# A later issue of block ends while the last chunk's exponentials are made, in a four-layer graph network

## The chip, the core and the metric

The kernel runs on one core of one Trainium2 chip. The metric is the device time of one execution in microseconds. Beside it stands one profiled execution, with the start, the length and the waits of every instruction. Engines are named as in the profile: PE is TensorE (PEld its weight loads), DVE is VectorE, ACT is ScalarE, POOL is GpSimd, and SP is SyncE, which here only issues transfers.

## What is computed

Four layers of a graph network run over 2708 nodes with 512 features. The adjacency matrix is sparse: about 16 neighbours in a row of 2708. Each layer ends in `x = layernorm(x + layer(x))`. Layers 0, 1 and 3 are products with the adjacency and a weight. Layer 2 is the one that matters here. It is two attention layers in a row:

```python
def _gat_layer(x, W, adj):
    proj = x @ W
    Wh, Ws = jnp.split(proj, 2, axis=-1)
    scores = Wh @ Ws.T
    a = jax.nn.softmax(scores, axis=-1) * adj
    out = a @ Wh
    out = out + x
    return jax.nn.leaky_relu(out, NEG_SLOPE)

for l in range(W_stack.shape[0]):
    x = _gat_layer(x, W_stack[l], adj)
```

## The kernel before

**Blocks and chunks.** The 2708 rows are cut into 22 blocks of 128 rows (the last has 20). They are worked on in six chunks, of four, four, four, four, three and three blocks. The attention of one chunk (a `Chunk`, named by attention layer and number, such as 1_3 for chunk 3 of the second attention layer) goes through these stages:

- *Scores* (tiles `sp`, `s`): for each of the 22 blocks of neighbours, PE multiplies a 128-row block against the chunk's columns; ScalarE copies the result, VectorE keeps the running maximum (`top`).
- *Shift* (`shift_rows`, `shift_columns`): the maximum of each column is spread over the partitions by transposes.
- *Softening* (`soften`, steps v = 0 to 22): VectorE subtracts the shift from block v and ScalarE takes the exponential. In the same call, for block v - 1, VectorE adds to the sum (`sum`), multiplies with the mask (`a`), and SyncE writes the result into a table in memory (`pairs`) beside the projected rows. For the last chunk a step is three VectorE operations of 128 x 276.
- *List sums* (`fetch`, `weigh`): since a row has few neighbours, the product with the masked exponentials is made from lists. GpSimd gathers 128 table rows for one list by an indirect transfer (tile `g`), and PE multiplies the gathered weights with the gathered rows into one PSUM bank (`acc`). A full block has twelve lists: four single ones, and eight in two groups of four (quads), each list of a quad on a quarter of the columns. Gathers run at most ten lists ahead in eleven buffers, and each product frees its buffers. A chunk's gathers begin when its softening is issued in full.
- *End* (`end`): VectorE scales the bank by the reciprocal sum, adds the row (`xr`), applies the leaky relu (`r`). In the first attention layer SyncE then writes the row, and 8 us after a chunk's last end its four blocks are turned by PE transposes (`turn`) and written. In the second attention layer VectorE adds the layer's own input and takes the statistics, five operations in all; 2 us after a chunk's last end comes `normalize`, and 4 us later the rest of it, which puts the rows into `made`.

**The order of issue.** Every engine's order is fixed by the order in which the program issues (class `Ordered`). The attention is planned while the program is written out. `Attention.clock` is the planner's clock: each piece of PE work advances it by an assumed cost (4 x columns / 2400 us for a product, 0.853 us for a single list, 1.1 for a quad). `later(us, what)` puts a call into `pending`, to be run by the first `advance` that reaches its time. A list product is issued by `weigh()` when its gather is thought to have landed, or at once with `weigh(True)`. In the main loop of `layer` softening of one chunk is mixed with the scores of the next and with list products of the chunk before that.

**The last chunk.** When a layer's scores are all issued, only the last chunk's shift and softening are left, with list products of chunks 3 and 4. After each softening step `until(done, fill)` issues list products, or pieces of `fill`, until the clock reaches the step's time. For the first attention layer `fill` is the next one's projection (`second`: tiles `mix`, `wst`, `z`). For the second it is the start of layer 3 (`Fast.early`): products `acc<-m,xh` and `acc<-m,xl` in groups of four blocks. For these, `prepare` makes the mask copies `m` and the two halves `xh`, `xl` of each row on ScalarE and VectorE. At its second piece that fill asks for rows 12 to 15 with `need(15)`:

```python
def need(self, i):

    while i not in self.made:
        if not self.weigh(True):
            self.pending.pop(0)[1]()
```

Rows 12 to 15 are chunk 3; blocks 16 to 18 are chunk 4, blocks 19 to 21 chunk 5. After group 3 of a chunk of layer 3, the four banks are copied out by ScalarE (`begun`), and the next chunk's group 0 uses those banks.

Of the kernel before, what the change touches and what calls it, by code (L numbers as in the profile page):

```python
# [53 lines left out]
class Ordered:  # L54


    def __init__(self, tc):
        self.tc, self.last = tc, {}
        for name in ("tensor", "vector", "scalar", "gpsimd", "sync"):
            setattr(self, name, OrderedEngine(self, getattr(tc.nc, name)))  # L60
# [27 lines left out]
class Kernel:  # L88
# [129 lines left out]
    def attention(self, before, after):  # L218

        nc, tc, small = self.nc, self.tc, self.small  # L220
        with ExitStack() as ctx:
# [100 lines left out]
            for layer in range(2):  # L322
                w = self.load_w(wpool, self.w2[layer], 2 * D, f"w_2{layer}")
                for i in range(NB):
                    ps = self.transposed(ps_tr, x[i], f"x{i}")
                    xt = turned.tile([P, DC, P], FP, tag="t", name=f"xt{i}")
                    nc.scalar.copy(xt, ps)
                    ws = rows.tile([P, D], FP, tag="row", name=f"ws{i}")
                    nc.vector.tensor_copy(ws, self.times_w(ps_mm, xt, w, D, f"ws{i}"))
                    nc.scalar.copy(z[i], self.times_w(ps_mm, xt, w, 0, f"wh{i}"))  # L330
                    n = rows_of(i)
                    ps = self.transposed(ps_tr, ws, f"ws{i}")
                    nc.vector.tensor_copy(wst[:, :, i * P : i * P + n], ps[:, :, :n])

                mx = scores(0)
                rden = softmax(0, mx)
                for i in range(NB):
                    if i + 1 < NB:
                        mx = scores(i + 1)
                    acc = weigh(i)  # L340
                    finish(i, acc, rden, layer == 1)
                    if i + 1 < NB:
                        rden = softmax(i + 1, mx)


    def general(self):
# [106 lines left out]

        given = [self.x_in[bass.ts(i, P), :] for i in range(NB)]
        layer(0, given, self.w0, None, self.b0, end0)
        layer(1, self.saved[0], self.w1, dis, self.b1, end1)
        self.attention(self.saved[1], self.saved[2])
        layer(3, self.saved[2], self.w3, None, self.b3, end3)

    def other_weights(self):  # L460
# [27 lines left out]
def cost(columns):  # L488

    return 4 * columns / 2400  # L490
# [894 lines left out]
class Attention:  # L1385
# [7 lines left out]
    def __init__(self, fast):  # L1393
        self.f, self.k, self.nc = fast, fast.k, fast.nc
        self.page, self.bank = fast.page, fast.bank
        tc = self.k.tc
        self.scratch = self.k.ctx.enter_context(
            tc.tile_pool(name="pairs", bufs=1, space=DRAM)
        )

        self.pairs = [
            [
                self.scratch.tile([NP, 2 * PAIR + D], FP, tag=f"p{a}{b}", name=f"pairs{a}{b}")
                for b in range(2)
            ]
            for a in range(2)
        ]
        self.mixed = self.scratch.tile([DC, P, D], FP, tag="mixed", name="mixed")  # L1410
        self.layers = [AttentionLayer(a, self.pairs[a]) for a in range(2)]
        self.clock, self.fetch_free, self.pending = 0.0, 0.0, []


    def blank(self):
# [316 lines left out]
    def weigh(self, wait=False):  # L1732

        nc = self.nc
        self.fetch_ahead()
        ch = next((c for c in self.chunks if c.to_weigh), None)
        if ch is None:
            return False
        q, ts, first, last = ch.to_weigh[0]
        if len(ch.fetched) < len(ts):  # L1740
            return False
        if ch.fetched[len(ts) - 1][1] > self.clock and not wait:
            return False
        ch.to_weigh.pop(0)
        if ch.rden is None:
            self.divisor(ch)
        w = ch.blocks[q][2]
        gs = [ch.fetched.pop(0)[0] for _ in ts]
        if first:
            ch.acc = self.bank(1, f"acc{ch.name}_{q}")  # L1750
        for h, g in enumerate(gs):
            lo, m = (0, w) if len(gs) == 1 else (h * QW, QW)
            e, z = (0, P - lo) if q % 2 else (D + lo, 0)
            nc.tensor.matmul(
                ch.acc[lo : lo + m],
                g[:, e : e + m],
                g[:, z : z + D],
                start=first,
                stop=last,
            )  # L1760
        self.advance(cost(D) if len(gs) == 1 else 1.1)
        if last:
            a = (ch, q, ch.acc, ch.x.pop(q), ch.first.pop(q, None))
            self.later(1.5, lambda: self.end(*a))
        self.fetch_ahead()
        return True

# [59 lines left out]
    def layer(self, ly, chunks, fill):  # L1827
        f = self.f
        self.chunks, self.made = chunks, {}
        for k, ch in enumerate(chunks):  # L1830
            old = chunks[k - 1] if k else None


            js = [0, 1, 2, NB - 1, *range(3, NB - 1)]
            for n, j in enumerate(js):
                if old and n == 0:
                    self.load_masks(old)
                if old and n >= 3:
                    if n == 3 and k >= 3:
                        while chunks[k - 3].to_weigh:  # L1840
                            self.weigh(True)
                    for _ in range(1 + n % 2):
                        if old.softened <= NB:
                            self.soften(old)
                self.scores(ch, j)
                f.beat()
                if n == 14 and k:
                    f.packed(k - 1)
                if n == 4 and k + 1 < len(chunks):
                    self.load_moving(chunks[k + 1])  # L1850
                if k + 1 == len(chunks) and n in ((5, 11, 19) if ly.number == 0 else (5, 11)):
                    next(fill)
                if old and n == 0:
                    self.greatest(old, js[-1])
                if n:
                    self.greatest(ch, js[n - 1])

                for _ in range(3):
                    if not self.weigh():
                        break  # L1860
                if old and n == 1:
                    self.shift_rows(old)
                if old and n == 2:
                    self.shift_columns(old)
        last = chunks[-1]
        self.load_masks(last)
        self.greatest(last, js[-1])
        self.until(self.clock + 3, fill)
        self.shift_rows(last)
        if ly.number == 1:  # L1870

            next(fill)
        self.until(self.clock + 3, fill)
        self.shift_columns(last)

        done = self.clock + (2 if ly.number == 0 else 4)
        while last.softened <= NB:
            self.soften(last)
            done += 1.4
            self.until(done, fill)  # L1880
        while any(c.to_weigh for c in chunks):
            if not self.weigh() and not next(fill, False):
                assert self.weigh(True)
        while self.pending:
            if not next(fill, False):
                self.pending.pop(0)[1]()
        for _ in fill:
            pass
# [97 lines left out]
```

## Time and profile before

| what | us |
|---|---|
| median of three timed runs | 2321.81 |
| lowest and highest of them | 2318.35, 2332.58 |
| the profiled execution's own time | 2299.72 |
| its span, first to last instruction | 2297.7 |
| PE busy in the span | 2269.4 |
| DVE busy | 1391.5 |
| POOL busy | 705.4 |
| ACT busy | 675.5 |

The profiled execution is shorter than the timed ones. Nearly every group of instructions shows the same line, L71, since the helper that fixes the order issues them all, so groups are told apart by their tiles (`out<-in`). The last softening of the first attention layer lies at about 1263 to 1302 us of the span, that of the second at about 1957 to 2017 us.

### The profile page before, as it was taken

What the parts mean: (1) busy time and instruction counts of PE and PEld (TensorE: products, weight loads), DVE (VectorE), ACT (ScalarE), POOL (GpSimd) and SP (SyncE); (2) the same over time, 40 slices, a digit from 0 to 9 for tenths busy, and PEclk for the clock granted to TensorE, in tenths of its full rate; (3) what the DMA queues carried; (4) which work ended last, traced back from release to release, by engine and by line L of the source; (5) the groups of instructions that cost most, each with busy time, mean ns of one, the idle gap of its engine ahead of it and who ended that gap; (6) DMA issues with size and microseconds to landing.
All of it is one profiled execution on the core that took longest, in us unless ns stands there. A gap on an engine that the chain in (4) does not pass through costs nothing.

```text
span 2297.7 us, 25903 instructions
## 1 busy us (share of the span) xinstructions
PE 2269.4 (99%) x8525; PEld 1289.0 (56%) x8525; DVE 1391.5 (61%) x2803; ACT 675.5 (29%) x1354; POOL 705.4 (31%) x822
## 2 busy tenths in 40 slices
PE   9999999999999999999999999999999999899997
PEld 6776876777644444443555444444443555466685
DVE  6777787786553537748667511238769788525523
ACT  7444452322111123223322200113223334342211
POOL 3433431111000001635557540001635467442000
PEclk9999999999999999999999999999999999999999
DMA  9966752223547415858789997405868799963311
GB/s 351 286 188 184 199 168 81 76 81 104 208 184 267 144 25 184 303 191 297 254 311 360 349 412 284 183 8 179 303 218 286 254 322 339 334 217 120 116 51 43
DMA packets 260929, 486.34 MB, mean 212 GB/s; under 512 B 40238, under 2 KB 126950, under 8 KB 260784
## 3 DMA queue, kind: packets, MB, share of 16 engines
q1 hardware_dynamic: 192128, 269.63, 33.6%
q0 software_dynamic: 68656, 214.96, 28.0%
q8 instruction: 69, 1.13, 0.2%
q14 instruction: 76, 0.62, 0.1%
HBM read 307.55 MB, written 176.92 MB: 211 GB/s over the span
## 4 chain that ended last, share of the span: by engine, by line
PE 86%; DMA 6%; DVE 4%; ACT 1%; issue 1%; POOL 1%; SPq 0%; ACTq 0%; POOLq 0%; DVEq 0%
PE sp L71 33%; PE acc L71 30%; PE mm L71 8%; PE z L71 6%; PE wst L71 6%; DMA x<-x 2%; DMA x<-in_x 1%; DMA at<-in_adj_t 1%; DMA g<-pairs,givers 1%; PE mix L71 1%; DMA pairs<-s 1%; POOL xt L71 1%; PE list L71 1%; ACT m L71 1%; PE tr_x2t L71 0%
## 5 line engine op out<-in xcount | busy, mean ns | idle before, releaser
L71 PE MATMUL sp<-xs,wst_sb 128*128 128x512 f32 (+3 forms) x2112 | 798.3, 544 | 0.0
L71 POOL DMA_INDIRECT g<-pairs,givers x510 | 524.2, 1028 | 872.9 <-issue 338.9
L71 PEld LDWEIGHTS sp<-xs,wst_sb 128*128 128x128 f32 (+1 forms) x2112 | 379.7, 186 | 408.4 <-issue 324.8
L71 PE MATMUL acc<-m,xh 128*128 128x512 f32 (+4 forms) x1584 | 566.8, 379 | 6.6 <-ACT m L71 5.1
L71 PE MATMUL acc<-m,xl 128*128 128x512 f32 (+4 forms) x1584 | 549.6, 365 | 2.0 <-DVE xl L71 1.8
L71 PEld LDWEIGHTS acc<-m,xh 128*128 128x128 f32 (+1 forms) x1584 | 288.0, 188 | 70.9 <-issue 21.3
L71 PEld LDWEIGHTS acc<-m,xl 128*128 128x128 f32 (+1 forms) x1584 | 288.3, 188 | 46.3 <-issue 5.3
L71 PE MATMUL acc<-g 128*32 128x512 f32 (+1 forms) x1020 | 264.8, 606 | 4.6 <-DMA g<-pairs,givers 4.0
L71 ACT COPY s<-sp 128x512 f32<-128x512 f32 (+2 forms) x252 | 132.7, 528 | 396.8 <-PE sp L71 395.1
L71 ACT ACTIVATE s<-s 128x512 f32<-128x512 f32 (+3 forms) x264 | 151.6, 580 | 319.8 <-DVE s L71 319.5
L71 DVE TENSOR_TENSOR top<-top,s 128x512 f32<-128x512 f32 (+2 forms) x240 | 149.1, 621 | 156.1 <-ACT s L71 154.5
L71 PE MATMUL mm<-w,ht 128*128 128x512 f32 (+1 forms) x528 | 223.7, 593 | 0.0
L71 ACT CAST m<-at 128x512 fp32r<-128x512 uint8 (+5 forms) x396 | 199.2, 567 | 62.3 <-DMA at<-mask 19.7
L71 DVE TENSOR_TENSOR s<-s,shift 128x512 f32<-128x512 f32 (+3 forms) x264 | 162.7, 620 | 36.2 <-ACT shift L71 36.2
L71 DVE TENSOR_TENSOR s<-s,a 128x512 f32<-128x512 f32 (+3 forms) x264 | 165.8, 628 | 13.6 <-DMA a<-mask 4.5
L71 DVE TENSOR_TENSOR sum<-sum,s 128x512 f32<-128x512 f32 (+4 forms) x252 | 156.5, 621 | 15.4 <-ACT s L71 15.4
L71 PEld LDWEIGHTS mm<-w,ht 128*128 128x128 f32 (+1 forms) x528 | 95.8, 186 | 117.0 <-issue 112.2
L71 PEld LDWEIGHTS acc<-g 128*32 128x32 f32 (+1 forms) x1020 | 74.6, 134 | 148.0 <-issue 116.5
L71 PE MATMUL z<-w,xt 128*128 128x512 f32 (+1 forms) x352 | 151.0, 596 | 0.0
L71 PE MATMUL wst<-xt,mixed 128*128 128x512 f32 (+2 forms) x384 | 150.5, 544 | 0.0
L71 POOL DMA_DIRECT2D x<-o x44 | 26.0, 597 | 329.7 <-DVE o L71 325.4
L71 PEld LDWEIGHTS wst<-xt,mixed 128*128 128x128 f32 x384 | 72.0, 190 | 71.1 <-issue 58.8
(168 smaller groups left out, 1476.7 us busy)
## 6 DMA issues: line engine op xcount, KB each, us to landing
pairs<-z_sb SPq DMA_DIRECT2D x84, 768.0 KB
pairs<-s SPq DMA_DIRECT2D x168, 256.0 KB
at<-in_adj_t SPq DMA_DIRECT2D x84, 256.0 KB
xres<-x POOLq DMA_DIRECT2D x44, 256.0 KB, 4.6
x<-o POOLq DMA_DIRECT2D x43, 256.0 KB, 3.4
pairs<-s SPq DMA_DIRECT2D x84, 128.0 KB
x<-x SPq DMA_DIRECT2D x37, 256.0 KB
at<-mask SPq DMA_DIRECT2D x32, 256.0 KB
```

Source lines behind the costliest of these rows:

```text
L71: ins = call(*args, **kw)
```

## The change

A flag `ending` is set when a layer's scores are all issued, and cleared when the last softening step of the last chunk is issued. While it is set, the end of a block is put 7 us of the planner's clock behind the block's last list product instead of 1.5. A product counts by the moment at which it is issued.

```diff
         self.clock, self.fetch_free, self.pending = 0.0, 0.0, []
+        self.ending = False
...
         if last:
             a = (ch, q, ch.acc, ch.x.pop(q), ch.first.pop(q, None))
-            self.later(1.5, lambda: self.end(*a))
+
+            self.later(7 if self.ending else 1.5, lambda: self.end(*a))
         self.fetch_ahead()
...
-        last = chunks[-1]
+        last, self.ending = chunks[-1], True
         self.load_masks(last)
...
             self.until(done, fill)
+        self.ending = False
         while any(c.to_weigh for c in chunks):
```

## The prediction

> **What bounds the kernel now.** I read the page first: busy shares and the chain that ended last.
>
> ```profile
> span 2297.7 us, 25903 instructions
> PE 2269.4 (99%) x8525; PEld 1289.0 (56%) x8525; DVE 1391.5 (61%) x2803; ACT 675.5 (29%) x1354; POOL 705.4 (31%) x822
> PE 86%; DMA 6%; DVE 4%; ACT 1%; issue 1%; POOL 1%; SPq 0%; ACTq 0%; POOLq 0%; DVEq 0%
> ```
>
> TensorE is the bound, 86% of the last chain; what takes nothing from it or its waits is free. Then the two places where the flag is on, by busy time in stretches (the first numbers are the stretch, its length and PE's busy time).
>
> ```profile
> 1240.00:1310.00 70.00, 69.75 (x228) 32.37 (x227) 37.59 (x90) 17.84 (x41) 41.01 (x42) 1.00 1.01 358
> 1958.40:1978.10 19.70, 16.45 (x34) 3.51 (x33) 6.96 (x17) 5.33 (x9) 14.82 (x17) 1.00 1.03 413
> 1992.80:2001.40 8.60, 4.52 (x10) 2.34 (x9) 7.24 (x17) 5.88 (x12) 2.73 (x5) 0.64 0.59 172
> 2001.40:2008.80 7.40, 5.93 (x26) 4.55 (x24) 6.53 (x17) 4.36 (x10) 1.00 (x1) 0.96 0.82 254
> ```
>
> In the first attention layer (ending at 1251 to 1302 us) PE never waits. In the second (1943 to 2017) it does. In 1958.4 to 1978.1 it runs 16 lists (the 33 weight loads, two for each list) in 19.7 us, 1.23 each, as gathers land; its order of weight loads shows the cause:
>
> ```profile
> 1964.64 0.14 PEld L71 LDWEIGHTS acc<-g 128*32 128x32 f32 x2 [0.85 <-DMA g<-pairs,givers]
> 1966.42 0.14 PEld L71 LDWEIGHTS acc<-g 128*32 128x32 f32 x2 [1.65 <-DMA g<-pairs,givers]
> 1967.57 0.14 PEld L71 LDWEIGHTS acc<-g 128*32 128x32 f32 x2 [1.00 <-DMA g<-pairs,givers]
> ```
>
> GpSimd issues a gather every 1.26 us there (0.95 and a gap of 0.30), so PE goes at GpSimd's pace. VectorE meanwhile stands at the end of block 16, the first of chunk 4; its second line is the wait:
>
> ```profile
> 1961.74 0.17 DVE L71 TENSOR_SCALAR rs_v<-mv 128x4 f32<-128x4 f32 x1
> 1974.11 0.75 DVE L71 SCALAR_TENSOR_TENSOR xr<-acc,rden,xr 128x512 f32<-128x512 f32 x1 [12.20 <-PE acc L71]
> 1996.74 0.69 DVE L71 SCALAR_TENSOR_TENSOR xl<-x,xh 128x512 fp32r<-128x512 f32 x1 [0.18 <-ACT xh L71]
> ```
>
> Behind it stand the second softening step (1984.08) and everything after. PE pays later, at the fourth group of the next layer's products, and before the next chunk:
>
> ```profile
> 1997.27 0.80 PE L71 MATMUL acc<-m,xh 128*128 128x512 f32 x1 [4.08 <-ACT m L71]
> 2008.79 0.50 PE L71 MATMUL acc<-m,xh 128*128 128x512 f32 x1 [1.47 <-ACT begun L71]
> ```
>
> [...] one end held VectorE 12.20 us with ready softening behind it. [...] behind the 4.08 us gap the granted clock averages 0.64 over 8.6 us. Gather waits of at most 2.1 us set off nothing.
>
> **The change part by part.** An end is one scheduled call on the planner's clock, which I followed by hand from the costs in the code; it does not advance that clock. So weighing and filling keep their order unless somebody waits for the end itself. Five ends are registered while the flag is on.
>
> *First attention layer: two ends.* The last of chunk 3 (1270.61 us, two VectorE operations, 1.4 us) goes some five softening steps down, and its turn, 8 later, goes from 655.7 to 660.9 on the clock (it is run at the first advance past its time). With it move 16 transposes (1.9 us of PE), 4 ScalarE copies, one row DMA and four turned DMAs of SyncE, past some ten pairs writes. They are read only when that chunk is projected, over 50 us later on the clock. The end of chunk 4's first block goes from 1302.28 to about 1312, behind two copies of z. Neither end stalled VectorE before, and PE is full with fill: zero gained. One bank fewer is free at the turn, which could hold PE for a ScalarE copy (0.6): I take +0.3, bounds 0 and 1.
>
> *Second attention layer: three ends, and a loop that waits for one.* The fill calls `need(15)` in mid-ending. That loop forces list products until block 15's row is made: its end, 2 later the normalizing, 4 later the rest. With 0 at block 15's last product, a single list advances 0.853, a quad 1.1:
> - Before: end due 1.5, run at 1.71; normalizing due 3.71, run at 4.51; rest due 8.51, run at 9.02. That is 4 singles, 2 quads, 4 singles: the 16 lists of the trace.
> - After: end due 7, run at 7.32; normalizing due 9.32, run at 10.12; rest due 14.12, run at 14.64. That is 4 singles, 2 quads, 4 singles, 2 quads, 4 singles: 28 lists. They are not short: chunk 4 has 36.
>
> So 12 more lists are forced at the pace of gathers: 12 x 1.23 = 14.8 us. Their own work (2 quads of 1.06, 4 singles of 0.86, 5.6 us) is taken from later, where PE was full. Net +9.2 before anything is won back. Block 16's end falls due at 5.61 + 7 = 12.61, still inside the loop and ahead of the rest, where it was before (at 7.32). VectorE's order there is unchanged, so the wait of 12.20 us **stays**. Only block 17's end is new in the ending (due 18.22), 3.1 us of VectorE after step 10.
>
> What is won back: PE now starts group 1 at 1978.1 + 14.8 = 1992.9; groups 1 and 2 took 14.9 us, so it reaches group 3 at 2007.8. That group's halves come later too. Step n is filled up until 4.3 + 1.4n, and the preparation of group 3 follows the four passes (1.71 each) of group 1: at 9.02 + 6.83 = 15.85 before, behind step 9; at 14.64 + 6.83 = 21.47 after, behind step 13. VectorE from 1996.1: one step of 1.19, the end 3.1, three steps 3.6, four xl 3.8: 2007.8. A tie: the gap and the half clock (1993.0 to 2007.2 for group 3, 14.1 us; its 32 matmuls at 0.227 are 7.3) go, 6.9 back. Next late: the four casts for the next chunk, behind step 18. 2004.0 + 3.8 + 5 x 1.19 = 2013.8, casts 2.2, copy 0.6: 2016.6. Before, that chunk began at 2008.79: +7.8. Less the 5.6 of work already done: **+2.2**. Bounds: 0, if GpSimd's pace loosens while the other DMA traffic drops; +9.2, with nothing won back. The twelve extra gathers (337 KB each by the queue's bytes) share the DMA engines with the row writes and pairs writes; at 413 GB/s and a share of 1.03 there is no slack, so I add nothing for gain.
>
> Chunk 5's gathers may now be issued some 12 us earlier by the clock; its last step ends near 2020 and its first product comes near 2040, with the 6.1 us (median) of a gather's landing between. PE is full from 2008.8 on, so this gains nothing. The flag's own statements issue nothing.
>
> **Sum.** 2297.7 + 2.5 = 2300.2 us of span; execution 2299.72 + 2.5 = 2302.2. The three timed runs have a median of 2321.81, 22 above the profiled execution, so I put the difference on the median: 2324.3.
>
> **Rivals.** A is the forecast, 0.55.
>
> B, slower: the extra forced gathers are not won back. One mechanism, in `need(15)`: for it speaks that 12 lists x 1.23 are certain once the loop is longer; against it that group 3 waited on softening which PE now gives time. It decides if group 3's last half is made after about 2015. 2321.8 + 9.2 + 0.3 = 2331.3. It passes 1% (some 23 us) only if lists came every 2.4 us ((23 + 5.6) / 12); the longest single distance between two lists in the trace is 2.2. Chance 0.2.
>
> C, faster: the change does what it says in the second layer too, and softening starts without the 12.20 us wait; both gaps close: 6.9 + 1.6 = 8.5 off, 2313.3. For it: that wait is the largest of VectorE there. Against: the order above. Chance 0.12.
>
> D, nothing: the loop runs dry of gathered lists and serves the pending calls at once, so the end is not late at all: 2321.8 to 2322.1. Against: each product frees a buffer and fetches the next. Chance 0.13.
>
> **How the numbers follow.** About 1% is what a measurement of this kernel can tell from no change. All four cases lie inside it, so same has 0.92; slower keeps 0.05 for a stall that the page pool's changed order might set off, faster 0.03. The three runs spread over 14 us, which widens the range: 2312 to 2337 takes in A, D, most of B and C.
>
> **What would show it.** Right: between the first softening step and group 1's products PE runs 28 lists, not 16; VectorE's long wait for block 16 is still there; no 4 us gap before group 3. Wrong: 16 lists there (D); softening steps ahead of block 16's end on VectorE (C); a gap before group 3 still there (B); any PE wait in the first layer's ending.

## The result, and the profile after

| kernel | median us | lowest to highest |
|---|---|---|
| before | 2321.82 | 2314.21 to 2336.82 |
| after | 2326.24 | 2316.61 to 2338.3 |

Each had twenty timed runs. The ratio after to before is 1.0011, with a 95% interval of 0.9993 to 1.0029: from 0.07% faster to 0.29% slower, no change that can be told. The prediction was 2324.3 us, 2.5 above the kernel before, which is a ratio of 1.0011 too. That the two agree to the fourth digit is luck: the interval reaches from 1.6 us below the kernel before to 6.7 above it.

The page of the kernel after, its span, the busy times by engine, and the shares by engine of the chain that ended last:

```profile
span 2327.4 us, 25894 instructions
PE 2286.3 (98%) x8525; PEld 1293.8 (56%) x8525; DVE 1390.9 (60%) x2803; ACT 674.4 (29%) x1354; POOL 707.4 (30%) x822
PE 88%; DMA 4%; DVE 3%; issue 2%; POOL 1%; ACT 1%; another core or an unknown queue 0%; SPq 0%; ACTq 0%; POOLq 0%; DVEq 0%
```

TensorE is still the bound. This one profiled span is 29.7 us longer than the one before (2297.7), and about half of that lies where the change does nothing: the scores of the first attention layer began 5.7 us later in it and took 497.3 us instead of 489.1. So the traces are compared by stage, and within the stage that the change touches.

The forced loop first. Weight loads (PEld) of the list products in the timeline of the kernel after; start, duration, and in brackets the idle time ahead and what ended it. Four of the 28 lists that run between 1981.26 and 2021.97:

```profile
1981.26 0.30 PEld L71 LDWEIGHTS acc<-g 128*128 128x128 f32 x2 [1.45 <-issue]
...
1989.02 0.14 PEld L71 LDWEIGHTS acc<-g 128*32 128x32 f32 x2 [1.06 <-DMA g<-pairs,givers]
...
2010.06 0.14 PEld L71 LDWEIGHTS acc<-g 128*32 128x32 f32 x2 [1.07 <-DMA g<-pairs,givers]
...
2020.88 0.50 PEld L71 LDWEIGHTS acc<-g 128*128 128x128 f32 x2 [1.35 <-DMA g<-pairs,givers]
```

There are 28 lists instead of 16, and most of them wait for a gather of their own. VectorE's timeline in the same stretch:

```profile
1985.56 0.17 DVE L71 TENSOR_SCALAR rs_v<-mv 128x4 f32<-128x4 f32 x1
2003.54 0.75 DVE L71 SCALAR_TENSOR_TENSOR xr<-acc,rden,xr 128x512 f32<-128x512 f32 x1 [17.81 <-PE acc L71]
...
2024.60 0.74 DVE L71 SCALAR_TENSOR_TENSOR xr<-acc,rden,xr 128x512 f32<-128x512 f32 x1
```

The wait at the end of block 16 did not go: it grew from 12.20 to 17.81 us. The end of block 17 (2024.60) stands between softening steps and waits for nothing.

It was not block 16's own lists that made it grow. These lines of PE's timelines hold the block's last lists, first before, then after (start, duration):

```profile
1969.79 4.28 PE L71 MATMUL acc<-g 128*32 128x512 f32 x8 [1.18 <-DMA g<-pairs,givers]
```

```profile
1991.91 5.10 PE L71 MATMUL acc<-g 128*32 128x512 f32 x10 [1.85 <-issue]
```

Before, they ended at 1974.07, and VectorE went on 0.04 us later (1974.11). After, they ended at 1997.01 by PE's records, and VectorE went on at 2003.54, 6.5 us later; without that the wait would have been 11.3. So in this trace the release by a finished list reaches the waiting engine late, or PE's records run early; no run here decides which.

Behind the loop TensorE (PE) has no more waits: its timeline shows two last long waits within the loop, and then none until 2070, where the kernel before had one of 4.08 and one of 1.47 us:

```profile
2014.42 1.10 PE L71 MATMUL acc<-g 128*128 128x512 f32 x2 [3.32 <-DVE sum L71]
2017.28 5.54 PE L71 MATMUL acc<-g 128*128 128x512 f32 x6 [1.75 <-DMA g<-pairs,givers]
```

Stages of PE in the second attention layer's ending, from the timelines (us). The loop runs from chunk 4's first sum product (`den`) to the first product of group 1; group 3 takes in the gap ahead of the next chunk; the rest is what follows until layer 3's first `mm` product:

| stage | before | after |
|---|---|---|
| forced loop (lists) | 20.5 (16) | 42.9 (28) |
| groups 1 and 2 with the gap ahead of group 3 | 19.2 | 15.2 |
| group 3 with the gap behind it | 11.5 | 7.3 |
| rest | 101.9 | 95.9 |
| sum | 153.1 | 161.3 |

The loop costs 22.4 us more; 4.0 and 4.2 come back at the groups and 6.0 in the rest. That leaves 8.2 us in these two executions; the timed medians differ by 4.4.

### The profile page after: what moved, and what is told of

Its sections match the earlier page's. It is cut to its first block, busy times and chain, and to the rows that moved or that the text cites. A ratio compares the mean times of both kernels' runs of the same rounds, so it can differ in the third digit from the quotient of the medians.

```text
span 2327.4 us, 25894 instructions
## 1 busy us (share of the span) xinstructions
PE 2286.3 (98%) x8525; PEld 1293.8 (56%) x8525; DVE 1390.9 (60%) x2803; ACT 674.4 (29%) x1354; POOL 707.4 (30%) x822
## 4 chain that ended last, share of the span: by engine, by line
PE 88%; DMA 4%; DVE 3%; issue 2%; POOL 1%; ACT 1%; another core or an unknown queue 0%; SPq 0%; ACTq 0%; POOLq 0%; DVEq 0%
PE sp L71 33%; PE acc L71 32%; PE mm L71 8%; PE z L71 6%; PE wst L71 6%; DMA g<-pairs,givers 1%; POOL g L71 1%; DMA at<-in_adj_t 1%; DMA x<-in_x 1%; PE mix L71 1%; PE list L71 1%; PE tr_x2t L71 0%; ACT m L71 0%; ACT xh L71 0%
## 5 line engine op out<-in xcount | busy, mean ns | idle before, releaser
L71 PE MATMUL acc<-g 128*32 128x512 f32 (+1 forms) x1020 | 276.1, 616 | 12.4 <-issue 4.6
```

What stands on the lines that cost most here:

```text
L71: ins = call(*args, **kw)
```

## The experiments

The first four ran on one chip beside 52 runs of the kernel before (median 2321.14 us), the last three on another beside 25 (2304.51 us). Each ratio is against the kernel before on its own chip. In the expectations A is the forecast's account; the other letters are explained in them.

**The change in one layer at a time.** `e1_first_only`:

```diff
-            self.later(7 if self.ending else 1.5, lambda: self.end(*a))
+            self.later(7 if self.ending and ch.ly.number == 0 else 1.5, lambda: self.end(*a))
```

> The 7 us hold in the first attention layer alone (two of the five ends). Theory A (the cost is the longer forced loop of the second layer): nothing moves, ratio to the kernel before 1.000 within 0.001; the forced stretch of the second layer runs 16 lists in some 20 us. Rival E (the first layer's moved turn and end cost something, since the change's profile has a stage there 6 us longer than before): ratio above 1.001, and the stage between the last score of the first layer and the first of the second is 210 us or more instead of 207.

Measured: 2320.71 us, ratio 0.9999 (0.998 to 1.0018). The first layer's half costs nothing that can be told, and the second layer's loop has its 16 lists, in 17.0 us. The end of the first layer took 210.4 us in this trace against 206.9 before and 213.0 after, as the rival expected; but it took 211.3 in `e4_need_serves`, which has the old first layer, and 206.6 in `e5_late_served`, which has the new one. That stage varies by some 5 us whatever the code, so it decides nothing.

`e2_second_only` has `ch.ly.number == 1` in that place.

> The 7 us hold in the second attention layer alone. Theory A: the whole of the change's cost is here, ratio 1.001 to 1.003 (2 to 7 us); 28 forced lists in 35 to 43 us, no gap of 4 us ahead of group 3. Rival E: ratio 1.000 or less, the second layer pays its gathers back in full.

Measured: 2325.08 us, ratio 1.0025 (1.0006 to 1.0045). The cost is in the second layer. VectorE's timeline of this kernel shows the long wait at block 16, which again goes on after the block's last list has ended in PE's records (1987.93):

```profile
1995.53 0.75 DVE L71 SCALAR_TENSOR_TENSOR xr<-acc,rden,xr 128x512 f32<-128x512 f32 x1 [20.60 <-PE acc L71]
```

Its loop has 28 lists and takes 42.9 us too, and it ends as in the kernel after, with one late gather. PE's timeline, the last three waits of the loop:

```profile
2004.54 1.12 PE L71 MATMUL acc<-g 128*128 128x512 f32 x2 [0.81 <-DMA g<-pairs,givers]
2009.20 1.65 PE L71 MATMUL acc<-g 128*128 128x512 f32 x2 [3.53 <-DMA g<-pairs,givers]
2011.10 2.08 PE L71 MATMUL acc<-g 128*128 128x512 f32 x2 [0.25 <-issue]
```

**The delay only where nobody asks.** `e3_chunk4_only` delays the ends of chunk 4 in the second layer and leaves the last one of chunk 3, for which `need(15)` polls, at 1.5:

```diff
-            self.later(7 if self.ending else 1.5, lambda: self.end(*a))
+            self.later(7 if self.ending and ch.ly.number == 1 and ch.k == 4 else 1.5, lambda: self.end(*a))
```

> The 7 us hold for chunk 4's ends in the second attention layer alone, so that the loop that asks for row 15 stays as short as before (16 lists), while block 16's end leaves VectorE's way. Theory A (the delay helps where nobody asks for the end): VectorE no longer stands 12 us at block 16, group 3's halves are made some 8 us earlier, the gap ahead of group 3 and the half clock go: 4 to 8.5 us less than before, ratio 0.996 to 0.998. Rival F (the page pool or the rows' way through memory holds ScalarE and softening anyway, as two waits on pages in the profile before hint): ratio 1.000, gap ahead of group 3 still 3 us or more.

Measured: 2312.84 us, ratio 0.9959 (0.9945 to 0.9974), faster than before and a little below A's range. The end of block 16 has moved behind the first softening steps, and VectorE no longer stands there. Its timeline:

```profile
1972.24 0.72 DVE L71 SCALAR_TENSOR_TENSOR xr<-acc,rden,xr 128x512 f32<-128x512 f32 x1
...
1993.23 0.74 DVE L71 SCALAR_TENSOR_TENSOR xr<-acc,rden,xr 128x512 f32<-128x512 f32 x1
...
2000.20 0.69 DVE L71 SCALAR_TENSOR_TENSOR xl<-x,xh 128x512 fp32r<-128x512 f32 x1 [0.18 <-ACT xh L71]
```

The loop has its 16 lists again (19.2 us), groups 1 and 2 take 15.4, group 3 takes 7.3 and the rest 101.8: 143.7 against 153.1 before, 9.4 off. The medians differ by 8.3. That the two figures are near each other should not be leaned on: ahead of the loop this execution has a PE wait of 4.40 us where the profile of before has 1.84 (`e1_first_only`, with the old second layer, has 4.38), and counted from the layer's last score the ending takes 167.3 us against 170.8. The gain is shown by the medians, the two closed gaps and VectorE's timeline.

**The loop changed instead of the delay.** `e4_need_serves` keeps the delay of 1.5 and makes `need` issue only the products of the chunk that is asked for, and then run what is pending, however early:

```diff
     def need(self, i):
+        asked = next(c for c in self.chunks if any(b[0] == i for b in c.blocks))
+        while asked.to_weigh:
+            self.weigh(True)
         while i not in self.made:
-            if not self.weigh(True):
-                self.pending.pop(0)[1]()
+            self.pending.pop(0)[1]()
```

> The delay is 1.5 everywhere as before, but the loop that asks for row 15 issues only chunk 3's own products and then serves the pending end and normalizing at once: 0 lists of chunk 4 are forced instead of 16. Theory A (each forced list costs PE its wait for the gather): 16 x 1.23 - 9.0 = 10.7 us of waits go, of which up to 7 may come back as a wait for group 3's rows: 4 to 11 us less, ratio 0.995 to 0.998. Rival G (PE waits for group 3's rows and not for lists, so the lists only fill the time): ratio 1.000, with a gap of 10 us or more ahead of group 2 or 3.

Measured: 2310.22 us, ratio 0.995 (0.9935 to 0.9966). No list of chunk 4 is forced. The price is small: rows 12 to 15 come late. The first line is ScalarE's timeline, the second PE's:

```profile
1987.02 0.63 ACT L71 ACTIVATE xh<-x 128x512 fp32r<-128x512 f32 x1 [5.19 <-DMA x<-x]
```

```profile
1991.21 0.49 PE L71 MATMUL acc<-m,xh 128*128 128x512 f32 x1 [1.24 <-ACT m L71]
```

ScalarE waits 5.19 us for a row that comes back from memory, and PE waits four times in group 3's first products, 2.7 us in all (0.57, 0.30, 1.24 and 0.55).

`e5_late_served` has the change as it is, with the same new `need`:

> The change as it is (7 us in both layers), but the loop that asks for row 15 serves the pending end and normalizing as soon as chunk 3's own products are issued: 0 forced lists of chunk 4. Theory A (the late end costs only through the loop that waits for it): as the same loop with the delay of 1.5, ratio 0.994 to 0.996. Rival E (the lateness itself costs, by a bank, a page or a later turn): 2 us or more slower than that, ratio 0.997 or more.

Measured: 2295.72 us, ratio 0.9967 (0.9953 to 0.9982), between the two expectations, with an interval that reaches into both. It overlaps that of `e4_need_serves`. With the new loop the change costs 0.17% by the two ratios, with the old one 0.11%, and neither is told from nothing. So this pair does not show that the change loses by the loop; it shows that the loop costs either kernel 0.4 to 0.5%. Where the change loses is shown by `e2_second_only` and `e3_chunk4_only`: they differ in nothing but the last end of chunk 3, for which the loop waits, and their medians lie 12.2 us apart.

**A longer delay.** `e6_delay12` delays by 12 in the second layer alone. All 36 lists of chunk 4 are then issued in the loop:

```diff
-            self.later(7 if self.ending else 1.5, lambda: self.end(*a))
+            self.later(12 if self.ending and ch.ly.number == 1 else 1.5, lambda: self.end(*a))
```

> 12 us instead of 7, in the second attention layer alone: by the planner's clock the loop then forces all 36 lists of chunk 4 (28 at 7 us, 16 at 1.5) before the pending calls are served. Theory A: 8 more lists of quads at 1.23 to 1.4, less their own work of 2.1: 8 to 9 us above the 7 us kernel, ratio 1.004 to 1.007; forced stretch 52 us or more. Rival H (what the loop takes is all paid back beyond a point, so the cost is set by something else than the count): ratio as at 7 us, 1.001 to 1.003.

Measured: 2312.0 us, ratio 1.0031 (1.0018 to 1.0044). That is below A's range and at the upper edge of the other, with an interval that reaches A's lower end. The eight further lists cost only 1.6 us of loop: 44.5 for 36 lists, 1.24 each, where 28 took 42.9. So more lists are not simply more time at one pace. What differs is seen in PE's timeline of this kernel: its lists last from 1966.26 to 2010.02, and its longest wait is one of 1.65 us:

```profile
1989.74 1.05 PE L71 MATMUL acc<-g 128*32 128x512 f32 x2 [0.98 <-DMA g<-pairs,givers]
1992.43 3.12 PE L71 MATMUL acc<-g 128*32 128x512 f32 x6 [1.65 <-DMA g<-pairs,givers]
...
2003.77 3.95 PE L71 MATMUL acc<-g 128*32 128x512 f32 x8 [0.25 <-DMA g<-pairs,givers]
2007.92 2.17 PE L71 MATMUL acc<-g 128*32 128x512 f32 x4 [0.20 <-DMA g<-pairs,givers]
2010.02 0.50 PE L71 MATMUL acc<-m,xh 128*128 128x512 f32 x1
```

**Both cures, and the rows handed over in SBUF.** `e7_rows_direct` takes the new `need`, the delay of `e3_chunk4_only`, and for rows 12 to 15 takes the tiles just made instead of reading them back from memory:

```diff
+            if t == 1:
+                for j in range(*GROUPS[3]):
+                    ly.rows[j] = self.attention.made[j]
             self.load(*seq[t + 2])
```

> Three edits together: the loop serves the end at once (0 forced lists), the 7 us hold for chunk 4's ends alone, and layer 3's group 3 takes rows 12 to 15 from the tiles that the normalizing made, instead of from memory after a write and a load. Theory A: without the way through memory the waits ahead of groups 2 and 3 shrink by up to 6 us: ratio 0.992 to 0.995. Rival J (the pages that the rows keep delay other copies by as much): ratio 0.995 to 0.997.

Measured: 2295.78 us, ratio 0.9962 (0.9944 to 0.998), outside A's range and inside the rival's, with an interval that reaches into A's. The second layer's whole ending, from its last score on, is the shortest of all (159.5 us; 170.8 before, 164.5 in `e5_late_served`), but the time does not show it. PE waits in small pieces on the mask copies now. From its timeline:

```profile
1976.17 0.50 PE L71 MATMUL acc<-m,xh 128*128 128x512 f32 x1 [0.95 <-ACT m L71]
1978.02 0.78 PE L71 MATMUL acc<-m,xh 128*128 128x512 f32 x1 [1.11 <-ACT m L71]
```

The four kernels that spare the loop or VectorE (`e3`, `e4`, `e5`, `e7`) lie between 0.995 and 0.9967 with overlapping intervals. Each of them beats the kernel before by 0.3 to 0.5%; which is best stays open.

## Why the prediction was right, point by point

**The order of issue: right.** 28 lists in the loop, block 16's end inside it, block 17's end between softening steps with nothing to wait for, group 3 reached so late that its preparation is done: all four stand in the trace as they were worked out on the planner's clock. `e2_second_only` and `e3_chunk4_only` show the cause: the same delay costs 0.25% with chunk 3's last end in it, and gains 0.41% without.

**The first layer, +0.3: nothing found.** `e1_first_only` gives 0.9999. The sign that was named as wrong, a PE wait in the first layer's ending, does occur. PE's timeline of the kernel after:

```profile
1279.06 0.88 PE L71 MATMUL tr_mx<-ident,wide 128*128 128x128 f32 x3 [2.80 <-remote]
```

It stands ahead of the first of the moved ends, which VectorE runs at 1297.21. `e4_need_serves`, with the old first layer, has such a wait too (1.83), and `e5_late_served`, with the new one, has none. The ratio of `e1_first_only` leaves no room for a cost over 0.2%.

**"12 x 1.23 = 14.8 us": too small.** This is the term that was mis-sized: the loop grew by 22.4. Split from the timelines:
- From the first `den` to the first list it took 2.2 us instead of 1.1: +1.1.
- The last five intervals, from the list at 2010.06 to group 1 at 2021.97, took 11.9 us where five at 1.23 are 6.2: +5.7. Of this the 3.32 us wait is 3.1 more than the usual 0.2, and the rest is the next late gather (1.75) and the clock.
- The remaining 23 lists went at 1.25 (28.8 from 1981.26 to 2010.06), +0.5.

Together 14.8 + 7.3 = 22.1 of 22.4. With 28 lists at 1.23 instead the loop would have been as forecast. Stretches of the kernel after; the columns are the stretch, its length, busy us (instructions) of PE, PEld, DVE, ACT and POOL, the granted clock, the share of the DMA engines, GB/s:

```profile
2010.50:2014.40 3.90, 0.61 (x2) 0.01 (x1) 3.30 (x8) 2.66 (x4) 3.60 (x2) 1.00 0.88 287
2014.40:2018.00 3.60, 1.82 (x3) 0.80 (x4) 3.50 (x10) 1.26 (x4) 2.68 (x4) 0.68 1.06 369
2018.00:2022.00 4.00, 4.00 (x7) 1.11 (x5) 3.86 (x11) 1.45 (x4) 3.09 (x4) 0.50 1.00 352
```

PE works 0.61 us of the 3.9 to 2014.4, and then the clock falls to 0.68 and 0.50: the six matmuls of the last three lists take 5.54 us, 0.92 each, where those at 2014.42 took 0.55. The kernel before shows such a fall behind its gap of 4.08 us (ended at 1997.27): its clock is 1.00 from 1990 to 1993, and then, in the same columns:

```profile
1997.00:2001.50 4.50, 4.23 (x9) 2.43 (x10) 3.42 (x7) 3.77 (x8) 2.73 (x5) 0.50 0.70 203
```

The prediction counted on half clock for this gap, which goes, and did not ask whether a longer loop could make such a gap of its own. It did, 3.32 us in the kernel after and 3.53 in `e2_second_only`, at the 25th and the 27th list, and the clock fell behind both (to 0.56 from 2009.2 to 2013 in `e2_second_only`). The loop of `e6_delay12` has no such gap: its granted clock is 1.00 from 1965 to 2011, and its first 28 lists take 35.5 us (1966.26 to 2001.72) against 40.7 and 39.3. So the pace of the prediction holds without the gap and fails in both kernels that have it. (The prediction's clock of 0.64 over 8.6 us was read from a stretch that includes the gap of 4.08 us itself, so it is higher than the 0.50 behind that gap.)

The gap itself begins on GpSimd. Its timeline in the kernel after:

```profile
2006.15 0.95 POOL L71 DMA_INDIRECT g<-pairs,givers  x1 [0.30 <-issue]
2008.71 1.15 POOL L71 DMA_INDIRECT g<-pairs,givers  x1 [1.61 <-PE acc L71]
2010.17 2.92 POOL L71 DMA_INDIRECT g<-pairs,givers  x1 [0.30 <-PE acc L71]
```

The gather of 2008.71, for the 25th list, was issued 2.56 us behind the one ahead of it instead of 1.26: it waited 1.61 us for a list product. With eleven buffers in turn that should be the 14th, whose buffer it takes; but PE loaded the weights of the 14th more than 10 us before (PEld's timeline):

```profile
1998.21 0.30 PEld L71 LDWEIGHTS acc<-g 128*128 128x128 f32 x2 [0.73 <-issue]
```

So this seems to be a late release again, as at block 16. The gather of the 27th list in `e2_second_only` shows the same; the weights of the 16th list were loaded at 1991.39 there. GpSimd's timeline of that kernel:

```profile
2002.13 2.16 POOL L71 DMA_INDIRECT g<-pairs,givers  x1 [1.63 <-PE acc L71]
```

Why the releases come late stays open. In `e6_delay12`, which has no such gap, block 16's end goes on 0.04 us after its last list, as before.

The 25th list came at 2014.39, 4.5 us behind the end of its gather's issue. The next gather took 2.92 us to issue, and its list came at 2017.27. The releaser that the trace puts beside the 3.32 us (a `sum`) is not what a list product needs.

**Won back, 6.9 us at group 3: about right.** From the last product of group 2 to the first of group 3, start to start, it was 4.5 us and is 0.2, and with the half clock (0.50 behind the gap before) 6.5 came back (8.2 less the 1.7 that follows). **The next chunk's casts as the next late thing: too careful.** Ahead of that chunk 1.9 us became 0.2; the prediction let it stand. It does stand in `e2_second_only` (2.6), so this term can fall either way. **The lists' own work taken from later, 5.6: right**, 6.0 less in the rest.

**The sum.** Loop +22.4, back 8.2 and 6.0: +8.2 in these profiles, where the same steps of the prediction made +2.2: the loop cost 7.6 more than forecast, and only 1.6 more came back. Measured by the medians it is +4.4, and +3.9 for `e2_second_only` alone. Whether every execution has the gap of 3.3 us, one profile of each kernel cannot say; with it in some only, the medians would lie between, as they do.

**The rivals.** B (not won back) comes near the 8.2 with its 9.2, but by luck: it has the same price for the loop as A, 14.8, and both gaps closed. C (softening starts without the wait) is what `e3_chunk4_only` does: its 8.3 us off the median are near C's 8.5, once chunk 3 is left out of the delay. In the change itself softening stands behind block 16's end in VectorE's order of issue, and VectorE waited 17.81 us there. D (the loop runs dry) did not happen: lists are there, one gather at a time.

## What to carry to other kernels

Ends that were put off cost nothing that could be told where nobody asked for them (0.9999 in the first layer); the one that a loop polls for cost 12.2 us (`e2_second_only` against `e3_chunk4_only`). So look for every loop that waits for the call, count what it issues meanwhile, and serve the request instead of filling time. Delay only what nobody asks for: the same delay, kept to the ends of chunk 4 that no loop polls for, was worth 0.4%. And when a stretch becomes bound by a transfer, look for the single longest gap in it as well as its mean pace, since behind the two gaps here (3.32 and 3.53 us) the clock was 0.50 and 0.56, and the gap was paid for again.

## What the runs showed of the hardware

- In the loop a gather's issue on GpSimd takes 0.95 to 1.34 us, but 2.92 once in the kernel after (2010.17) and 2.16 once in `e2_second_only`. Both times VectorE was making `xl`. But `e6_delay12` makes the same `xl` at 1986.5 to 1988.4 while gathers issue in 0.95 to 1.03 us, and in the kernel after one of 2.24 us (1835.94) runs beside softening and no `xl`, so no run here shows that this is the cause. It stays open.
- Half clock came behind waits of different lengths. In the loop before, the longest gather wait between matmuls is 1.18 us (the prediction's "at most 2.1 us" lay between weight loads), and the clock is 1.00 in every stretch of 2 us from 1957 to 1985. The kernel after has a wait of 1.85 us in the loop (ended at 1991.91), and the clock is 0.71 and 0.50 over the next two stretches of 2 us; in `e2_second_only` it is 0.50 from 1974 to 1978 behind a wait of 2.74. In `e4_need_serves` the products behind a wait of 1.56 (ended at 1979.81) start every 0.43 us from 1980.30 to 1983.29, where those from 1974 to 1975.9 start every 0.23; in `e6_delay12` a wait of 1.65 does nothing (clock 1.00 from 1990 to 2000). So the length of one wait does not decide it; what does, no run here shows. While the lists waited for gathers, a slow clock cost little: the first 23 went at 1.25 us with two such stretches among them (0.50 from 1983 to 1985 and from 1993 to 1995).
- The ending of the first layer, in kernels with the same code there, took 206.1 to 211.3 us from one execution to another. Differences of a few us between two single profiles say little unless they come with a line that explains them.
